# An eighth of a softmax's tokens moved onto the partitions in a four-layer fused network

## The chip, the cores and the metric

One NeuronCore of a Trainium2 chip runs the whole network in one program. The metric is device time in microseconds; three runs of the kernel before took 5653.28, 5671.16 and 5692.56 us, a median of 5671.16. The engines are called PE (TensorE; PEld is its weight load), DVE (VectorE), ACT (ScalarE), POOL (GpSimd) and SP (SyncE, which here only issues DMAs).

## The reference

Sixteen images of 64x64 tokens (4096) with 256 channels pass through four layers. Each layer first normalises its input over 32 groups of channels and adds its result to it. Layer 0 replaces each token by the nearest of 1024 codes, layer 1 is a row-wise attention with a sigmoid, layer 3 a linear attention of four heads with a layer norm. The change concerns layer 2:

```python
    def _L2_conv_ref(x, w1, b1, w2, b2, w3, b3):
        ...
        n = h * w
        xf = x.reshape(b, n, c)
        x0 = jnp.einsum('bnc,c->bn', xf, w1) + b1[0]
        x1 = jnp.einsum('bnc,c->bn', xf, w2) + b2[0]
        x2 = jnp.einsum('bnc,c->bn', xf, w3) + b3[0]
        sim = x0[:, :, None] * x1[:, None, :]
        sm = jax.nn.softmax(sim, axis=1)
        feats = jnp.einsum('bn,bnm->bm', x2, sm)
        gate = jax.nn.sigmoid(feats).reshape(b, h, w, 1)
        return gate * x
```

For each token m, a softmax over all 4096 tokens n of the product x0[n] * x1[m] weighs x2[n]. So an image needs 4096 x 4096 exponentials, their sum over n (the denominator) and their sum weighted with x2 (the numerator).

## The kernel before

The kernel is written with Tile: the code allocates tiles from pools and issues instructions, and a scheduler puts in the waits and fixes the order on each engine. Each layer of each image is a Python generator (stats0 L313, stage1 L329 for layer 0, layer1 L441, rows2 L567, stage2 L620 and gate2 L681 for layer 2, stage3 L717). A generator yields a number after each step, and the main loop at the end interleaves all generators by these numbers: each task has a start and a length in units of one image, so that in the middle of the run layer 0 of one image, layer 1 of the one before, layer 2 of an earlier one and layer 3 of a still earlier one run side by side. Blocks marked as urgent (statistics, small weights) are moved ahead. The engines themselves take their instructions in the resulting order.

PSUM is split into two pools: ps_m with four single banks (`bank`, L70) for most products, and ps_w with two pairs of banks (`wide`, L73). The pairs are used by the search of layer 0 (pd, L403, 32 per image, read by DVE in L409), by layer 1's h (ph, L493, eight per image, read by ACT in L502) and by its output (po, L533, eight per image, read by DVE in L538).

Layer 2 in detail. rows2 computes the three rows x0, x1, x2 for all tokens (L593; four column groups of PE, 32 columns each), writes them to DRAM (L599) and transposes them so that x0 and x1 also stand with the token on the partition, as x01 with 32 tiles of 128 tokens (L602, L603). spread_rows (L610) loads half of the x0 row and half of the x2 row, 2048 tokens each, onto all 128 partitions (L615). stage2 first finds the largest and the smallest x0 (L626, L627, L629), and from them nmax, minus the largest exponent of each token m (L631, L632). Then, for each half of the tokens n and each of the 32 tiles T of tokens m, with m on the partitions and n along the free dimension:

```python
                    nc.scalar.activation(
                        ex, x0b, AF.Exp, bias=nmax[:, T : T + 1], scale=x01[:, T, 1:2], accum_out=den[:, h, T : T + 1]
                    )
                    nc.vector.tensor_tensor_reduce(
                        out=ex, in0=ex, in1=x2b, scale=1.0, scalar=0.0, op0=ALU.mult, op1=ALU.add,
                        accum_out=num[:, h, T : T + 1],
                    )
                    yield 2.4
```

So ACT forms the exponentials and the denominator (L645), DVE multiplies by x2 and forms the numerator (L648), 64 pairs of 2048 columns per image. The sums of both halves give the gate (L656 to L663), which is transposed and stored (L666 to L669). For the last image stage2 runs in eight parts of four tiles T, so that its gate2 can start early.

Other lines that the prediction's steps name: the Identity of layer 0's search (L398), the index search (L414), the gather of codes (L415, an indirect DMA on POOL's queue), layer 1's narrow products (L482) and the bf16 product that adds a bias row (L498), layer 3's key maximum, exponential and context (L754, L774, L803, L809, L813), its transposes (L902) and its output copy (L913).

## Time and profile before

The profiled execution took 5674.06 us, of which the span from the first to the last instruction is 5672.1 us.

| what | value |
|---|---|
| three runs, median | 5671.16 us (5653.28 to 5692.56) |
| profiled execution, span | 5674.06 us, 5672.1 us |
| instructions | 76096 |
| mean granted PE clock | 0.962 of full speed |
| DMA | 1059.26 MB, mean 187 GB/s |
| DVE, layer 2's numerator (L648) | 2360.4 us, 1024 instructions |
| ACT, layer 2's exponentials (L645) | 2138.6 us, 1024 instructions |
| ACT, reading their sums (L645) | 194.4 us, 1024 instructions |
| PE, the search's products (L403) | 1971.1 us, 4096 records |
| DVE, the search (L409 and L414) | 619.9 and 622.9 us, 512 instructions each |
| ACT, the search (L398) | 582.5 us, 512 instructions |

How to read it: the profile gives for each engine the time in which it was busy, and for each group of instructions (line, engine, operation) the busy time, the mean duration of one and the idle time of the engine ahead of them. Matmuls are pipelined, so the records of PE overlap and a busy PE isn't PE at its peak. A product of f32 operands on PE appears as two records. The time of an image in the middle of the run is read from the instruction that occurs once per image, POOL's reduction over partitions (L629): it starts at 1624.26, 1947.51, 2279.78, 2612.22, 2947.67, 3283.12, 3623.10, 3957.20, 4288.91, 4622.80 and 4948.66 us, and for the last image at 5220.89 us.

### The profile page before, as it was taken

What the parts mean: (1) busy time and instruction counts of PE and PEld (TensorE: products, weight loads), DVE (VectorE), ACT (ScalarE), POOL (GpSimd) and SP (SyncE); (2) the same over time, 40 slices, a digit from 0 to 9 for tenths busy, and PEclk for the clock granted to TensorE, in tenths of its full rate; (3) what the DMA queues carried; (4) which work ended last, traced back from release to release, by engine and by line L of the source; (5) the groups of instructions that cost most, each with busy time, mean ns of one, the idle gap of its engine ahead of it and who ended that gap; (6) DMA issues with size and microseconds to landing.
All of it is one profiled execution on the core that took longest, in us unless ns stands there. A gap on an engine that the chain in (4) does not pass through costs nothing.

```text
span 5672.1 us, 76096 instructions
## 1 busy us (share of the span) xinstructions
PE 5162.0 (91%) x26927; PEld 3189.6 (56%) x26927; DVE 5049.3 (89%) x7186; ACT 4571.1 (81%) x6642; POOL 1801.5 (32%) x1076
## 2 busy tenths in 40 slices
PE   7977889989999999999999999999999999987788
PEld 3534446545656566565655656565565656564556
DVE  7589799899999999999999999999999999988882
ACT  4468589888989898888978888898888879887873
POOL 2223234323333333334333333333333333321221
PEclk9988999999999999999999999999999999998889
DMA  8553744655665757566575656657575675745543
GB/s 254 174 178 84 232 115 144 214 163 185 196 198 175 224 159 236 171 211 198 185 234 155 216 185 200 210 173 236 160 224 183 201 219 156 222 149 176 200 157 119
DMA packets 521365, 1059.26 MB, mean 187 GB/s; under 512 B 52504, under 2 KB 266392, under 8 KB 512792
## 3 DMA queue, kind: packets, MB, share of 16 engines
q1 hardware_dynamic: 406288, 885.11, 46.5%
q0 software_dynamic: 73728, 67.14, 8.3%
q10 hardware_dynamic: 40968, 102.13, 4.6%
q8 instruction: 214, 3.51, 0.3%
q14 instruction: 167, 1.37, 0.1%
HBM read 751.18 MB, written 303.04 MB: 186 GB/s over the span
## 4 chain that ended last, share of the span: by engine, by line
PE 46%; DVE 17%; ACT 16%; issue 6%; DMA 5%; POOL 4%; SPq 0%; ACTq 0%; DVEq 0%; POOLq 0%
PE pd_s L403 14%; ACT ex_s L645 7%; DVE ex_s L648 7%; PE ph_l L493 4%; PE pxo_s L908 3%; PE pqv_s L782 3%; PE po_l L533 2%; PE pk_s L765 2%; ACT nn_s L398 2%; POOL qv_s L802 2%; PE pz_s L857 2%; DVE i_s L414 2%; DVE nn_s L409 2%; PE pxo_s L902 2%; PE pvr_s L865 2%
## 5 line engine op out<-in xcount | busy, mean ns | idle before, releaser
L648 DVE CUSTOM_DVE_ANT_0 ex_s<-ex_s,x2b 128x2048 f32<-128x2048 f32 x1024 | 2360.4, 2312 | 77.6 <-ACT ex_s L645 74.6
L645 ACT ACTIVATE ex_s<-x0b,nmax_s,x_r 128x2048 f32<-128x2048 f32 x1024 | 2138.6, 2089 | 40.7 <-DVE num_s L648 30.5
L403 PE MATMUL pd_s<-e,xn_s 128*128 128x512 f32 x4096 | 1971.1, 614 | 43.9 <-DVE m L409 27.9
L415 POOL DMA_INDIRECT xc_s<-in_emb_rows,i_s x512 | 1113.7, 2175 | 1852.7 <-DVE i_s L414 1337.5
L403 PEld LDWEIGHTS pd_s<-e,xn_s 128*128 128x128 f32 x4096 | 745.8, 195 | 778.8 <-issue 669.1
L409 DVE CUSTOM_DVE_ANT_0 nn_s<-pd_s,nn_s 128x1024 f32<-128x1024 f32 x512 | 619.9, 1212 | 113.5 <-PE pd_s L403 63.0
L414 DVE FIND_INDEX8 i_s<-m,nn_s 128x8 uint32<-128x1024 f32 x512 | 622.9, 1217 | 0.0
L398 ACT ACTIVATE nn_s<-ne,nx_s 128x1024 f32<-128x1024 f32 x512 | 582.5, 1143 | 33.1 <-DVE nx_s L369 18.7
L493 PE MATMUL ph_l<-wh_l,xt_l 128*128 128x256 f32 x2048 | 519.6, 390 | 28.7 <-DVE m L409 16.9
L782 PE MATMUL pqv_s<-wqv_s,xk_s 128*128 128x256 f32 x2048 | 489.3, 381 | 0.0
L493 PEld LDWEIGHTS ph_l<-wh_l,xt_l 128*128 128x128 f32 x2048 | 379.7, 192 | 138.9 <-issue 69.0
L782 PEld LDWEIGHTS pqv_s<-wqv_s,xk_s 128*128 128x128 f32 x2048 | 389.1, 191 | 120.6 <-issue 59.7
L802 POOL TENSOR_TENSOR qv_s<-qv_s,qm_s 128x512 f32<-128x512 f32 x128 | 221.6, 1731 | 662.6 <-DVE qm_s L801 363.2
L868 POOL TENSOR_TENSOR lrs_s<-lrs_s,mhalf 128x4 f32<-128x4 f32 x128 | 178.0, 1391 | 677.2 <-ACT lrs_s L867 663.3
L756 POOL TENSOR_TENSOR qv_s<-qv_s,qd_s 128x512 f32<-128x512 f32 x128 | 214.4, 1675 | 249.0 <-DVE qd_s L755 132.0
L533 PE MATMUL po_l<-blk,h_l 128*128 128x128 f32 x2048 | 282.1, 288 | 3.0 <-DVE m L409 1.5
L533 PEld LDWEIGHTS po_l<-blk,h_l 128*128 128x128 f32 x2048 | 260.6, 200 | 41.1 <-issue 24.5
L908 PE MATMUL pxo_s<-wctx_s,qo_s 128*128 128x256 f32 x1024 | 269.2, 386 | 2.2 <-DVE qo_s L876 2.2
L765 PE MATMUL pk_s<-xk_s,wk_s 128*128 128x512 f32 x512 | 256.0, 620 | 1.0 <-DMA xk_s<-x_g 0.9
L913 ACT COPY y_s<-pxo_s 128x512 f32<-128x512 f32 x256 | 147.5, 580 | 132.4 <-PE pxo_s L912 116.0
L378 PE MATMUL pt_s<-ident,xc_s 128*128 128x128 f32 x1024 | 156.7, 282 | 105.2 <-DMA xc_s<-in_emb_rows,i_s 79.0
L351 ACT ACTIVATE sq_s<-xt_s,first 128x512 f32<-128x512 f32 x256 | 200.2, 806 | 37.2 <-DMA x0b<-rows_r 21.0
(206 smaller groups left out, 7322.0 us busy)
## 6 DMA issues: line engine op xcount, KB each, us to landing
xs_s<-in_xT SPq DMA_DIRECT2D x128, 512.0 KB
xt_s<-in_xT SPq DMA_DIRECT2D x128, 512.0 KB
xc_s<-in_x SPq DMA_DIRECT2D x128, 512.0 KB
x_s<-xt_s ACTq DMA_DIRECT2D x128, 512.0 KB
xt_l<-x_s SPq DMA_DIRECT2D x128, 512.0 KB
x_l<-xt_l SPq DMA_DIRECT2D x128, 512.0 KB
xr_r<-x_l SPq DMA_DIRECT2D x128, 512.0 KB
xg_g<-x_l SPq DMA_DIRECT2D x128, 512.0 KB
```

Source lines behind the costliest of these rows:

```text
L398: nc.scalar.activation(nn, ne2, AF.Identity, bias=nx2[ch][:, t : t + 1])
L403: nc.tensor.matmul(pd[:, cols], lhsT=xn[ch][:, k, t * P : (t + 1) * P], rhs=e2[:, k, cols], start=(k == 0), stop=(k == NK - 1),)
L409: nc.vector.tensor_tensor_reduce(out=nn, in0=pd, in1=nn, scale=1.0, scalar=-3.0e38, op0=ALU.add, op1=ALU.max, accum_out=m8[:, 0:1],)
L414: nc.vector.max_index(i8, m8, nn)
L415: nc.gpsimd.indirect_dma_start(out=xc[ch][:, t, :], out_offset=None, in_=emb_rows, in_offset=bass.IndirectOffsetOnAxis(ap=i8[:, 0:1], axis=0),
L493: nc.tensor.matmul(ph[:, t, :], lhsT=X[:, k, t * P : (t + 1) * P], rhs=wh_n[:, k, :], start=(t % 2 == 0 and k == 0), stop=False, skip_grou ...
L533: nc.tensor.matmul(po[:, m : m + P], lhsT=h[:, t, k * P : (k + 1) * P], rhs=at[:, t, :, :].rearrange("p r i -> p (r i)"), start=True, stop ...
L645: nc.scalar.activation(ex, x0b, AF.Exp, bias=nmax[:, T : T + 1], scale=x01[:, T, 1:2], accum_out=den[:, h, T : T + 1])
L648: nc.vector.tensor_tensor_reduce(out=ex, in0=ex, in1=x2b, scale=1.0, scalar=0.0, op0=ALU.mult, op1=ALU.add, accum_out=num[:, h, T : T + 1],)
L765: nc.tensor.matmul(pk, lhsT=wk_n[:, k, :], rhs=xt[:, k, :], start=(k == 0), stop=(k == NK - 1))
L782: nc.tensor.matmul(pqv[:, j, :], lhsT=xt[:, k, t * P : (t + 1) * P], rhs=wqv_n[:, k, :], start=(j == 0 and k == 0), stop=False, skip_group ...
L908: nc.tensor.matmul(px[:, j, :], lhsT=qT[:, t * P : (t + 1) * P], rhs=wctx[:, 1, :], start=False, stop=False, skip_group_check=True,)
```

## The change

Of the 32 tiles of 128 tokens n, the last four (SHARE = 4, an eighth) leave the loop over n along the free dimension. For them n lies on the partitions and m along the free dimension:

- rows2 now also keeps x2 in x01. stage2 gathers x1, nmax and the four tiles of x0 in one tile, transposes it (one PE product), and splits the 68 resulting rows into three bf16 parts each (five DVE instructions on PSUM). They go to DRAM in seven DMAs and come back as the two operands of a product with 12 rows: three rows for nmax against ones, nine for the products of the parts of x0 and x1. All these DMAs are issued on SP's queue.
- Per chunk of 512 tokens m (eight per image), `begin` loads the moving operand (four DMAs on SP, one per row group of PE). `outer`, twice, forms the exponents of two tiles of n in a pair of banks (two bf16 products in two row groups), and `powers` takes the Exp of the pair in one ACT instruction of 1024 columns. `contract` forms both sums over n by four f32 products onto 32 columns each, with x2 and ones as the weights, and copies the bank with ACT; `collect` transposes the result (four PE products) and adds the four groups (one DVE reduction).
- The exponentials and numerators of the second half become 1536 columns wide instead of 2048, and so do the loads of x0 and x2 for it.
- The pairs of banks come from ps_w, the others from ps_m. The two final sums of the gate become reductions over three terms.

The calls hang in the loop of stage2: of each eight steps, outer follows the exponential in steps 0 and 1, powers in steps 1 and 2, contract and the next begin stand in step 5, collect in step 7.

```diff
@@ -37,6 +37,9 @@
 LAG4 = 0.04
 LEN3 = {0: 0.4, 1: 0.33, 2: 0.37}
 FILL = ((0.05, 0.95, 2), (1.0, 1.27, 3), (1.4, 1.58, 2))
+SHARE = 4
+SHARES = {}
+PROD = 12
 EARLY = sum(n for _, _, n in FILL)
 
 
@@ -136,6 +139,14 @@
                 t[:, :512], lhsT=ones3, rhs=ones3.unsqueeze(1).to_broadcast([P, 4, P]), start=True, stop=True,
                 skip_group_check=True,
             )
+
+    spread = const.tile([P, 2, P], BF16, name="spread")
+    nc.gpsimd.memset(spread, 0.0)
+    for g in range(4):
+        nc.gpsimd.memset(spread[32 * g : 32 * g + PARTS], 1.0)
+    pair = const.tile([P, 8, 32], F32, name="pair")
+    nc.gpsimd.memset(pair, 0.0)
+    nc.gpsimd.memset(pair[:, :, 1], 1.0)
 
     h_row, qv_row, x_row = row_tile("h_row"), row_tile("qv_row"), row_tile("x_row")
 
@@ -581,7 +592,7 @@
                 )
             brow_n = small.tile([P, 1], F32, tag="brow_n", name=f"brow_{tag}")
             nc.scalar.activation(brow_n, pb[:, 0:1], AF.Identity, bias=brow)
-        x01 = small.tile([P, NT, 2], F32, tag="x01", name=f"x01_{tag}", bufs=2)
+        x01 = small.tile([P, NT, 3], F32, tag="x01", name=f"x01_{tag}", bufs=2)
         rd = dram.tile([3, 2, 4, CW], F32, tag="rows", name=f"rows_{tag}", bufs=3)
         for h in range(2):
             pr = bank(f"pr_{tag}_{h}")
@@ -602,20 +613,22 @@
                 nc.tensor.transpose(pt[:, t * P : (t + 1) * P], rows[:, t * P : (t + 1) * P], ident)
             nc.vector.tensor_copy(
                 x01[:, 16 * h : 16 * h + 16, :].rearrange("p (j t) n -> p j t n", t=CH),
-                pt.rearrange("p (t j n) -> p j t n", j=4, n=32)[:, :, :, 0:2],
+                pt.rearrange("p (t j n) -> p j t n", j=4, n=32)[:, :, :, 0:3],
             )
             yield 4
         rows_d[b] = x01, rd, [spread_rows(rd, b, 0)]
 
     def spread_rows(rd, b, h):
 
-        x0b = s2p.tile([P, TOK // 2], F32, tag="x0b", name=f"x0b_{b}_{h}", bufs=2)
-        x2b = s2p.tile([P, TOK // 2], F32, tag="x2b", name=f"x2b_{b}_{h}", bufs=2)
-        for dst, n in ((x0b, 0), (x2b, 2)):
+        width = TOK // 2 - (P * SHARES.get(b, SHARE) if h == 1 else 0)
+        both = []
+        for tag, n in (("x0b", 0), ("x2b", 2)):
+            dst = s2p.tile([P, TOK // 2], F32, tag=tag, name=f"{tag}_{b}_{h}", bufs=2)[:, :width]
             nc.sync.dma_start(
-                out=dst, in_=rd[n : n + 1, h, :, :].rearrange("o j n -> o (j n)").to_broadcast([P, TOK // 2])
+                out=dst, in_=rd[n : n + 1, h, :, :].rearrange("o j n -> o (j n)")[:, :width].to_broadcast([P, width])
             )
-        return x0b, x2b
+            both.append(dst)
+        return both
 
     def stage2(b, parts=1):
 
@@ -627,36 +640,136 @@
         nc.vector.tensor_reduce(ext[:, 1:2], x01[:, :, 0], AX.X, ALU.min, negate=True)
         ab = small.tile([P, 2], F32, tag="ab", name=f"ab_{tag}", bufs=1)
         nc.gpsimd.partition_all_reduce(ab, ext, P, bass_isa.ReduceOp.max)
-        nmax = small.tile([P, NT], F32, tag="nmax", name=f"nmax_{tag}", bufs=1)
+        K = SHARES.get(b, SHARE)
+        cat = small.tile([P, 2 * NT + 8], F32, tag="cat", name=f"cat_{tag}", bufs=1)
+        nmax = cat[:, NT : 2 * NT]
         nc.vector.tensor_scalar(nmax, x01[:, :, 1], ab[:, 0:1], -1.0, ALU.mult, ALU.mult)
         nc.vector.scalar_tensor_tensor(nmax, x01[:, :, 1], ab[:, 1:2], nmax, op0=ALU.mult, op1=ALU.min)
-        den = small.tile([P, 2, NT], F32, tag="den", name=f"den_{tag}", bufs=1)
-        num = small.tile([P, 2, NT], F32, tag="num", name=f"num_{tag}", bufs=1)
+        sums = small.tile([P, 2, 3, NT], F32, tag="sums", name=f"sums_{tag}", bufs=1)
         halves.append(spread_rows(rd, b, 1))
+
+        others, banks = {}, {}
+
+        def parts_of_rows():
+            nc.vector.tensor_copy(cat[:, 0:NT], x01[:, :, 1])
+            nc.vector.tensor_copy(cat[:, 2 * NT : 2 * NT + K], x01[:, NT - K :, 0])
+            nc.vector.tensor_copy(pair[:, 0:K, 0], x01[:, NT - K :, 2])
+            n = 2 * NT + K
+            pp = bank(f"pcat_{tag}")
+            nc.tensor.transpose(pp[:n, :P], cat[:, :n], ident)
+            bits = small.tile([2 * NT + 8, PARTS, P], BF16, tag="bits", name=f"bits_{tag}", bufs=1)
+            for m in range(PARTS):
+                nc.vector.tensor_copy(bits[:n, m, :], pp[:n, :P])
+                if m + 1 < PARTS:
+                    nc.vector.tensor_tensor(pp[:n, :P], pp[:n, :P], bits[:n, m, :], ALU.subtract)
+            ud = dram.tile([1 + PARTS, PARTS, NT, P], BF16, tag="ud", name=f"ud_{tag}")
+            nc.sync.dma_start(out=ud[0].rearrange("m t p -> t m p"), in_=bits[NT : 2 * NT])
+            for m in range(PARTS):
+                nc.sync.dma_start(out=ud[1 + m].rearrange("m t p -> t m p"), in_=bits[0:NT])
+            vd = dram.tile([PARTS, PARTS, 8, P], BF16, tag="vd", name=f"vd_{tag}")
+            for m in range(PARTS):
+                nc.sync.dma_start(out=vd[:, m, 0:K].rearrange("m t p -> t m p"), in_=bits[2 * NT : n])
+            for g in range(4):
+                nc.sync.dma_start(
+                    out=spread[32 * g + PARTS : 32 * g + PROD, 0 : K // 4, :],
+                    in_=vd.rearrange("i m (e g) p -> (i m) g e p", g=4)[:, g, 0 : K // 4, :],
+                )
+            return ud
+
+        def begin(c):
+            u = s2p.tile([P, CW], BF16, tag="uu", name=f"uu_{tag}_{c}", bufs=2)
+            src = ud.rearrange("i m t p -> (i m) (t p)")[:, c * CW : (c + 1) * CW]
+            for g in range(4):
+                nc.sync.dma_start(out=u[32 * g : 32 * g + PROD, :], in_=src)
+            others[c] = u
+
+        def outer(c, n):
+            e, q = divmod(n, 2)
+            if n == 0:
+                others[c] = [others.pop(c)]
+            u = others[c][0]
+            pw = wide(f"pet_{tag}_{c}_{n}")
+            for r in range(2):
+                g = 2 * q + r
+                rows = slice(32 * g, 32 * g + PROD)
+                nc.tensor.matmul(
+                    pw[:, r * CW : (r + 1) * CW], lhsT=spread[rows, e, :], rhs=u[rows, :], start=True, stop=True
+                )
+            banks[c, n] = pw
+
+        def powers(c, n):
+            e, q = divmod(n, 2)
+            if q == 0:
+                others[c].append(s2p.tile([P, TOK // 2], F32, tag="ex", name=f"et_{tag}_{c}_{e}", bufs=3))
+            nc.scalar.activation(others[c][-1][:, 2 * q * CW : 2 * (q + 1) * CW], banks.pop((c, n)), AF.Exp)
+
+        def contract(c):
+            pn = bank(f"pn_{tag}_{c}")
+            for e in range(K // 4):
+                for g in range(4):
+                    nc.tensor.matmul(
+                        pn[32 * g : 32 * g + 32, :], lhsT=pair[:, 4 * e + g, :],
+                        rhs=others[c][1 + e][:, g * CW : (g + 1) * CW], start=(e == 0), stop=(e == K // 4 - 1),
+                    )
+            nc.scalar.copy(others[c][-1][:, 0:CW], pn)
+
+        def collect(c):
+            row = others.pop(c)[-1]
+            pt = bank(f"pnt_{tag}_{c}")
+            for t in range(CH):
+                nc.tensor.transpose(pt[:, t * P : (t + 1) * P], row[:, t * P : (t + 1) * P], ident)
+            nc.vector.tensor_reduce(
+                sums[:, :, 2, c * CH : (c + 1) * CH].rearrange("p r t -> p t r"),
+                pt.rearrange("p (t j n) -> p t n j", j=4, n=32)[:, :, 0:2, :], AX.X, ALU.add,
+            )
+
+        if K:
+            ud = parts_of_rows()
+            begin(0)
         gd = dram.tile([NT, P], F32, tag="gate", name=f"gd_{tag}")
         gates_d[b] = gd
         yield 2
         rest = gate2(b) if parts > 1 else None
         for part in range(parts):
             those = range(part * NT // parts, (part + 1) * NT // parts)
+            step = 0
             for h, (x0b, x2b) in enumerate(halves):
                 for T in those:
-                    ex = s2p.tile([P, TOK // 2], F32, tag="ex", name=f"ex_{tag}_{h}_{T}", bufs=3)
+                    width = x0b.shape[-1]
+                    ex = s2p.tile([P, TOK // 2], F32, tag="ex", name=f"ex_{tag}_{h}_{T}", bufs=3)[:, :width]
                     nc.scalar.activation(
-                        ex, x0b, AF.Exp, bias=nmax[:, T : T + 1], scale=x01[:, T, 1:2], accum_out=den[:, h, T : T + 1]
+                        ex, x0b, AF.Exp, bias=nmax[:, T : T + 1], scale=x01[:, T, 1:2],
+                        accum_out=sums[:, 1, h, T : T + 1],
                     )
                     nc.vector.tensor_tensor_reduce(
                         out=ex, in0=ex, in1=x2b, scale=1.0, scalar=0.0, op0=ALU.mult, op1=ALU.add,
-                        accum_out=num[:, h, T : T + 1],
+                        accum_out=sums[:, 0, h, T : T + 1],
                     )
-                    yield 2.4
+                    yield 2.4 * width / (TOK // 2)
+                    c = part + step // 8
+                    n = step % 8
+                    if K == 0:
+                        pass
+                    elif n <= K // 2:
+                        if n > 0:
+                            powers(c, n - 1)
+                            yield 1.2
+                        if n < K // 2:
+                            outer(c, n)
+                    elif n == 5:
+                        contract(c)
+                        if c + 1 < NCHUNK:
+                            begin(c + 1)
+                    elif n == 7:
+                        collect(c)
+                    step += 1
             n = len(those)
             cols = slice(those[0], those[0] + n)
             gate = small.tile([P, NT], F32, tag="gate", name=f"gate_{tag}_{part}", bufs=1)[:, 0:n]
-            nc.vector.tensor_tensor(gate, den[:, 0, cols], den[:, 1, cols], ALU.add)
+            nc.vector.tensor_reduce(gate, sums[:, 1, 0 : 2 + (K > 0), cols].rearrange("p h t -> p t h"), AX.X, ALU.add)
             nc.vector.reciprocal(gate, gate)
             nsum = small.tile([P, NT], F32, tag="nsum", name=f"nsum_{tag}_{part}", bufs=1)[:, 0:n]
-            nc.vector.tensor_tensor(nsum, num[:, 0, cols], num[:, 1, cols], ALU.add)
+            nc.vector.tensor_reduce(nsum, sums[:, 0, 0 : 2 + (K > 0), cols].rearrange("p h t -> p t h"), AX.X, ALU.add)
             nc.vector.tensor_tensor(gate, gate, nsum, ALU.mult)
             nc.scalar.activation(gate, gate, AF.Exp, scale=-1.0)
             nc.vector.tensor_scalar(gate, gate, 1.0, None, ALU.add)
```

## The prediction

> **What bounds the kernel now.** I read the totals first, then the chain of waits, the busy times by stage, the costliest groups and the order of time on TensorE.
>
> ```profile
> PE 5162.0 (91%) x26927; PEld 3189.6 (56%) x26927; DVE 5049.3 (89%) x7186; ACT 4571.1 (81%) x6642; POOL 1801.5 (32%) x1076
> PE 46%; DVE 17%; ACT 16%; issue 6%; DMA 5%; POOL 4%; SPq 0%; ACTq 0%; DVEq 0%; POOLq 0%
> ```
>
> The first line is the busy time of each engine, the second the chain that ended last. No engine stands alone: TensorE and VectorE are both nearly full, ScalarE follows, and the chain runs through TensorE most. The stages, cut where an image's partition_all_reduce (L629, once per image) ran, show where that holds. Columns: window, length, then busy time and records of PE, PEld, DVE, ACT, POOL; the last row is one of the 200 us windows.
>
> ```profile
> 316.69:704.28 387.59, 301.95 (x1320) 154.41 (x1318) 335.16 (x466) 277.17 (x357) 108.68 (x59) 0.90 0.53 161
> 704.28:1624.26 919.98, 857.40 (x4492) 513.97 (x4492) 859.32 (x1179) 807.10 (x1132) 306.68 (x169) 0.97 0.57 175
> 1624.26:4948.66 3324.40, 3143.36 (x16787) 1959.55 (x16786) 3114.89 (x4410) 2840.94 (x4131) 1144.56 (x656) 0.99 0.63 196
> 5220.89:5672.10 451.21, 360.43 (x1728) 259.99 (x1726) 295.19 (x459) 283.37 (x468) 103.47 (x76) 0.88 0.46 155
> ...
> 1800.00:2000.00 200.00, 193.93 (x1031) 120.28 (x1030) 188.41 (x267) 168.57 (x245) 69.75 (x43) 0.98 0.69 217
> ```
>
> The stretch from 1624 to 4949 us is ten images of 332.4 us. Of each, PE is busy 314.3 us (94.6%), DVE 311.5 (93.7%), ACT 284.1 (85.5%). The 200 us window is the fullest that PE gets after the start: 97%.
>
> **What the change removes.** Layer 2's exponents of the second half of the tokens become 1536 wide instead of 2048, 32 pairs per image.
>
> ```profile
> L648 DVE CUSTOM_DVE_ANT_0 ex_s<-ex_s,x2b 128x2048 f32<-128x2048 f32 x1024 | 2360.4, 2312 | 77.6 <-ACT ex_s L645 74.6
> L645 ACT ACTIVATE ex_s<-x0b,nmax_s,x_r 128x2048 f32<-128x2048 f32 x1024 | 2138.6, 2089 | 40.7 <-DVE num_s L648 30.5
> L409 DVE CUSTOM_DVE_ANT_0 nn_s<-pd_s,nn_s 128x1024 f32<-128x1024 f32 x512 | 619.9, 1212 | 113.5 <-PE pd_s L403 63.0
> ```
>
> VectorE: the same operation takes 2.312 us at 2048 and 1.212 at 1024, 1.07 ns a column; 512 columns are 0.55 us, 17.6 us per image. ScalarE: exponentials take 2.089 us at 2048 and 0.628 at 512 (L803), 0.95 ns a column; 0.487 us each, 15.6 us per image.
>
> **What it adds on VectorE.** Eight reductions of 32 values per partition: between the copy of that size (L603, 0.174 us) and the reduction of 512 (L754, 0.678); nearer the copy, 0.2, so 1.6. Once per image the splitting of 68 rows into three bf16 parts: three copies (nearest L813, 0.292) and two subtractions (nearest L809, 0.340), with three small copies 2.1; the final sums, now reductions, 0.2. Together 3.9 (3.5 to 8), net -13.7 us per image.
>
> **On ScalarE.** Sixteen exponentials of 1024 columns from a pair of banks: the copy of that shape takes 1.013 (L502), the Exp of 512 from a bank 0.670 (L774), plus 0.487 is 1.16; I take 1.1, so 17.6. Eight copies of a bank at 0.58 (L913), 4.6. Net +6.6 (+5 to +8). At 85.5% ScalarE has room for it.
>
> **On TensorE.** Per image: sixteen bursts of two bf16 products with 12 rows and 512 columns (outer), eight bursts of four f32 products onto 32 columns each (contract), 32 transposes, one more for the parts. The rows are the order of time on PE (start, length, engine, line, operation, xcount; an f32 product is two records):
>
> ```profile
> 3705.43 1.07 PE L482 MATMUL pfg_l<-xt_l,wfg_l 128*32 128x256 f32 x16
> 3706.43 1.13 PE L493 MATMUL ph_l<-wh_l,xt_l 128*128 128x256 f32 x4
> 3707.40 0.38 PE L498 MATMUL ph_l<-h_row,ones 128*128 128x512 bf16 x1
> 3707.62 1.89 PE L493 MATMUL ph_l<-wh_l,xt_l 128*128 128x256 f32 x8
> ...
> 2593.82 1.94 PE L593 MATMUL pr_r<-xr_r,wrow_n 128*32 128x512 f32 x16
> 2595.69 2.84 PE L403 MATMUL pd_s<-e,xn_s 128*128 128x512 f32 x6
> ```
>
> A bf16 product of 512 columns holds PE 0.22 us (3707.40 to 3707.62; the rest of its 0.38 overlaps). The 16 narrow records of L482 hold it 1.00 where four at a time would stream 0.86, and the four full ones behind take 1.13 instead of 1.03 elsewhere: about 0.24 for going into the narrow form and out of it. Outer: 0.22 if the two row groups stream together, 0.43 if in turn, and 0.24 for the switch; I take 0.56, the middle of 0.46 and 0.67, 9.0 us per image. Contract: L593's 16 records hold PE 1.87, so eight 0.94 and the way out, 1.0; one after the other eight records of 0.43 are 3.4. L593 is the same shape in the same four column groups, so 1.0: 8 us per image. The transposes cost 0.44 per four (L902), with the one for the parts 3.8. Together 21 us per image. The lower bound, no switch and everything side by side, is 14; the upper, contract in turn and outer 0.67, is 42.
>
> [...]
>
> **Waits.** Each outer takes one of two bank pairs, so far used 48 times per image (32 by L403, 8 each by ph and po), now 64. The pair is held until ScalarE's exponential, which the code puts behind the next 2 us Exp, about one of the 64 steps of 332 us: 5 us. What queues behind a PE waiting for a pair is every stage's products. Today that wait is small (waits view: engine, line, releaser, total, times, longest):
>
> ```profile
> PE ph_l L493 <- DVE m L409: 13.7, 7, 2.0
> ...
> PE pd_s L403 <- DVE m L409: 1.4, 2, 1.1
> ```
>
> The two come to 1.5 us per image in the stretch; I put a growth of 2 us inside the margin below. SP gets 43 more issues per image, at about 0.37 us each (the nearest rows) 16 us, and two store-then-load waits, where today such a wait (x0b on its rows) totals 43.1 us in 24 times, 1.8 each. Behind them stand the loads of the search, layer 1 and layer 3. These load about two chunks ahead, a chunk being 332/8 = 41 us, so I cost it at nothing; with the cover gone, 10 us per image, 160 in all. GpSimd gets only memsets at the start, 1 us.
>
> **The sum.** The profiled execution took 5674.1 us with a span of 5672.1, 3 us above the median of the three runs. In the stretch PE goes to 314.3 + 21 = 335.3 us, more than the whole period of 332.4. At the 97% of its fullest window that is 345.7, +13.3 over ten images: +133. From 704 to 1624 (three of 306.7, PE 285.8): 306.8/0.97 = 316.3, +9.6 three times: +29. From 317 to 704 and after 5221 PE is at 78 and 80% and the saved 13.7 us count; about half of it each, as VectorE is not alone there: -12. With the start +1: 5674 + 151 = **5825 us**. By its own bounds: 14 us instead of 21 gives 328.3/0.97 = 338.5, +61 and +7, less 12, 5730; PE no fuller than today's 94.6% gives 354.4, +220, and in the earlier stretch at 93.2% 329, +67, 5960; 42 us on PE at 97% gives 367 and 338, +350 and +94, about 6110.
>
> **Rivals.** *VectorE was the bound, and PE's busy time is slack (faster).* Records overlap: counting 0.43 us per 512 columns of an f32 record, 0.215 per 256 and so on, the products of one image need only about 297 us of PE, 89% of the period, and the rest is tails at waits. VectorE at 311.5 - 13.7 = 297.8 and today's 93.7% would allow 317.8. PE needs 297 + 14 = 311 at the least, which at 97% is 320.6: -12 for each of ten images, -11 for each of three, -30 at the ends: 5490. With 21 us it is 318/0.97 = 328, some -85 in all, 5590. Nearer the second I put it at **5580**. It decides if outer and contract cost PE less than about 17 us. Against it: the chain is 46% PE and 17% DVE, and PE in order of time runs for tens of us with no gap.
>
> [...]
>
> *It evens out.* 13.7 off VectorE, 21 onto an engine with 35 us of tails and idle per image: about **5670**.
>
> *Bank pairs.* Each second outer makes a product wait as long as the mean of the row above, 1.96 us: 16 us per image, +200 over thirteen, **6020**. It decides if pairs are held well over 5 us, because ScalarE gets behind.
>
> **How the numbers follow.** About 1% is what a measurement of this kernel can tell from no change: 5614 to 5728. Forecast (PE the bound) 0.56, of which 0.03 within 1%; VectorE the bound 0.22; even 0.12; bank pairs 0.10. So faster 0.22, same 0.15, slower 0.63. The range, 5570 to 6010, leaves out the lower half of the second case and what lies above PE no fuller than now: most of the bank pairs and contract in turn. The forecast's own range is 5730 to 5960.
>
> **What would show it.** Right: in the middle PE busy near 97%, DVE under 90%, a period near 346 us, contract about 1 us, DVE waiting for PE more than now. Wrong: a period under 330 with PE's records the same, or outer's two products starting together and nothing lost around them (faster); or a large wait of the search's products for the new exponential, or loads arriving late (slower still).

## The result and the profile after

Four runs of the changed kernel took 5979.96 to 5991.99 us, median 5990.2; four of the kernel before 5653.28 to 5692.56, median 5673.14. The ratio is 1.0552 [1.0521, 1.0583]: 5.5% slower, 317 us. The span of the profiled execution grew from 5672.1 to 5986.8 us.

Totals, chain and stages of the kernel after, with the same columns as before (stages: window, length, busy time and records of PE, PEld, DVE, ACT, POOL, then PE clock, DMA share, GB/s):

```profile
PE 5480.0 (92%) x28991; PEld 3291.3 (55%) x28991; DVE 4850.2 (81%) x7442; ACT 4673.2 (78%) x7026; POOL 1729.2 (29%) x1083
PE 52%; DVE 11%; ACT 8%; issue 4%; DMA 3%; POOL 1%; POOLq 0%; ACTq 0%; DVEq 0%; SPq 0%
```

```profile
319.10:712.36 393.26, 322.04 (x1457) 160.68 (x1457) 321.35 (x482) 286.15 (x384) 106.93 (x59) 0.90 0.53 159
712.36:1705.98 993.62, 917.05 (x4834) 533.73 (x4833) 818.41 (x1215) 817.42 (x1192) 286.11 (x168) 0.96 0.52 162
1705.98:4886.74 3180.76, 3006.83 (x16294) 1819.25 (x16292) 2704.62 (x4134) 2617.32 (x3940) 1010.36 (x592) 0.98 0.59 186
5456.08:5986.80 530.72, 436.60 (x2168) 304.18 (x2166) 332.35 (x545) 351.08 (x589) 96.13 (x85) 0.88 0.46 151
```

The third row of stages is nine images between the same reductions over partitions. The same nine images of the kernel before, for comparison, since the prediction's row held ten:

```profile
1624.26:4622.80 2998.54, 2834.70 (x15123) 1767.15 (x15122) 2812.95 (x3987) 2558.89 (x3723) 1029.64 (x592) 0.98 0.63 197
```

An image takes 353.4 us instead of 333.2, +20.2. Of the busy times of an image, PE grew by 19.1 us (315.0 to 334.1), DVE fell by 12.0 (312.6 to 300.5), ACT grew by 6.5 (284.3 to 290.8). PE's busy share is 94.5% in both. At first sight the time follows PE's work to the microsecond; the experiments show that this is a coincidence.

The 314.7 us of span by stage: up to the first image's reduction +2.4, the next stage +5.7, the three images +73.6 (24.5 each), the nine +182.2, the tenth +20.9 (325.9 to 346.8), and the two last together +29.8 (272.2 to 222.6 and 451.2 to 530.7).

The groups that answer to those of before, and the Exp of the pair of banks (busy time, mean ns, idle time ahead of it and its main releaser):

```profile
L744 DVE CUSTOM_DVE_ANT_0 ex_s<-ex_s,x2b 128x2048 f32<-128x2048 f32 (+1 forms) x1024 | 2073.2, 2034 | 157.8 <-ACT ex_s L740 156.7
L740 ACT ACTIVATE ex_s<-x0b,cat_s,x_r 128x2048 f32<-128x2048 f32 (+1 forms) x1024 | 1920.1, 1876 | 66.8 <-DVE sums_s L744 60.5
L420 DVE CUSTOM_DVE_ANT_0 nn_s<-pd_s,nn_s 128x1024 f32<-128x1024 f32 x512 | 621.8, 1215 | 300.4 <-PE pd_s L414 217.8
...
L704 ACT ACTIVATE et_s<-pet_s 128x1024 f32<-128x1024 f32 x256 | 260.6, 1019 | 81.7 <-PE pet_s L695 80.4
```

The removed work is gone as computed. VectorE waits more: its idle time ahead of the search went from 113.5 us (63.0 of it for PE's products) to 300.4 (217.8), and ahead of the numerators, nearly all for ACT's Exp, from 77.6 to 157.8. PE's waits in the nine images after:

```profile
PE pgt_s L779 <- DVE gate_s L776: 45.1, 9, 9.6
PE pt_s L389 <- DMA xc_s<-in_emb_rows,i_s: 28.1, 9, 3.6
...
PE pd_s L414 <- DVE m L420: 19.4, 17, 1.4
...
PE pet_s L695 <- DMA spread<-vd_s: 10.9, 9, 2.1
```

The first is new in this stretch: once per image, 5.0 us, PE stands at the transposition of the gate. The last is the new load of the weights of outer. Of the two bank-pair waits of the prediction's rows, pd for m has grown from 1.1 us in nine images to 19.4, and ph for m, 11.8 before, is gone.

The two new shapes in PE's order of time (start, length, engine, line, operation, records):

```profile
3303.68 0.39 PE L695 MATMUL pet_s<-uu_s,spread 12*128 12x512 bf16 x2
3304.05 3.70 PE L414 MATMUL pd_s<-e,xn_s 128*128 128x512 f32 x8
...
3328.24 1.06 PE L710 MATMUL pn_s<-et_s,pair 128*32 128x512 f32 x8
3329.24 0.65 PE L988 MATMUL pdv_s<-ident,lrs_s 128*128 128x128 f32 x4
```

From start to next start outer holds PE 0.37 us here and contract 1.00.

### The profile page after: what moved, and what is told of

The parts are those of the page before. It is cut to its first block, busy times and chain, and to the rows that moved or that the text cites. A ratio compares the mean times of both kernels' runs of the same rounds, so it can differ in the third digit from the quotient of the medians.

```text
span 5986.8 us, 81555 instructions
## 1 busy us (share of the span) xinstructions
PE 5480.0 (92%) x28991; PEld 3291.3 (55%) x28991; DVE 4850.2 (81%) x7442; ACT 4673.2 (78%) x7026; POOL 1729.2 (29%) x1083
## 4 chain that ended last, share of the span: by engine, by line
PE 52%; DVE 11%; ACT 8%; issue 4%; DMA 3%; POOL 1%; POOLq 0%; ACTq 0%; DVEq 0%; SPq 0%
PE pd_s L414 15%; DVE ex_s L744 5%; PE ph_l L504 4%; PE pqv_s L895 4%; PE pxo_s L1021 3%; ACT ex_s L740 3%; PE pk_s L878 3%; PE po_l L544 2%; PE pn_s L710 2%; PE pxo_s L1015 2%; PE pz_s L970 2%; PE pvr_s L978 2%; PE pc_s L920 2%; PE pfg_l L493 1%; DMA xc_s<-in_emb_rows,i_s 1%
## 5 line engine op out<-in xcount | busy, mean ns | idle before, releaser
L744 DVE CUSTOM_DVE_ANT_0 ex_s<-ex_s,x2b 128x2048 f32<-128x2048 f32 (+1 forms) x1024 | 2073.2, 2034 | 157.8 <-ACT ex_s L740 156.7
L740 ACT ACTIVATE ex_s<-x0b,cat_s,x_r 128x2048 f32<-128x2048 f32 (+1 forms) x1024 | 1920.1, 1876 | 66.8 <-DVE sums_s L744 60.5
L420 DVE CUSTOM_DVE_ANT_0 nn_s<-pd_s,nn_s 128x1024 f32<-128x1024 f32 x512 | 621.8, 1215 | 300.4 <-PE pd_s L414 217.8
L409 ACT ACTIVATE nn_s<-ne,nx_s 128x1024 f32<-128x1024 f32 x512 | 579.1, 1143 | 61.0 <-DVE nx_s L380 40.4
L981 POOL TENSOR_TENSOR lrs_s<-lrs_s,mhalf 128x4 f32<-128x4 f32 x128 | 201.6, 1575 | 666.5 <-ACT lrs_s L980 649.0
L915 POOL TENSOR_TENSOR qv_s<-qv_s,qm_s 128x512 f32<-128x512 f32 x128 | 169.8, 1326 | 746.4 <-DVE qm_s L914 527.2
L704 ACT ACTIVATE et_s<-pet_s 128x1024 f32<-128x1024 f32 x256 | 260.6, 1019 | 81.7 <-PE pet_s L695 80.4
L878 PE MATMUL pk_s<-xk_s,wk_s 128*128 128x512 f32 x512 | 274.2, 662 | 0.7 <-DMA xk_s<-x_g 0.7
L869 POOL TENSOR_TENSOR qv_s<-qv_s,qd_s 128x512 f32<-128x512 f32 x128 | 152.8, 1194 | 415.3 <-DVE qd_s L868 290.9
L544 PE MATMUL po_l<-blk,h_l 128*128 128x128 f32 x2048 | 265.5, 280 | 5.9 <-DVE m L420 3.2
L544 PEld LDWEIGHTS po_l<-blk,h_l 128*128 128x128 f32 x2048 | 247.0, 193 | 32.6 <-issue 17.2
```

Source lines behind the costliest of these rows:

```text
L409: nc.scalar.activation(nn, ne2, AF.Identity, bias=nx2[ch][:, t : t + 1])
L420: nc.vector.tensor_tensor_reduce(out=nn, in0=pd, in1=nn, scale=1.0, scalar=-3.0e38, op0=ALU.add, op1=ALU.max, accum_out=m8[:, 0:1],)
L544: nc.tensor.matmul(po[:, m : m + P], lhsT=h[:, t, k * P : (k + 1) * P], rhs=at[:, t, :, :].rearrange("p r i -> p (r i)"), start=True, stop ...
L740: nc.scalar.activation(ex, x0b, AF.Exp, bias=nmax[:, T : T + 1], scale=x01[:, T, 1:2], accum_out=sums[:, 1, h, T : T + 1],)
L744: nc.vector.tensor_tensor_reduce(out=ex, in0=ex, in1=x2b, scale=1.0, scalar=0.0, op0=ALU.mult, op1=ALU.add, accum_out=sums[:, 0, h, T : T ...
L878: nc.tensor.matmul(pk, lhsT=wk_n[:, k, :], rhs=xt[:, k, :], start=(k == 0), stop=(k == NK - 1))
```

## The experiments

Two theories at the start. *PE's work*: the time follows the 19 us of products that an image gets, and PE can't be filled further. *Waits*: the products could be borne, but what hangs on them (readers on ScalarE and VectorE, the gate, the loads) makes engines stand. Percentages of PE are its busy share in the nine images between the same reductions; "above" is the median above that of the kernel before measured with it.

**The relief alone.** The share is left out, and with it an eighth of the tokens of each sum.

```diff
-SHARE = 4
+SHARE = 0
-        width = TOK // 2 - (P * SHARES.get(b, SHARE) if h == 1 else 0)
+        width = TOK // 2 - (P * 4 if h == 1 else 0)
```

> The last four tiles of n are left out altogether: no share on TensorE, and the second half stays 1536 wide, so VectorE loses 17.6 us and ScalarE 15.6 us per image against the kernel before, TensorE nothing (the gate then lacks an eighth of its sums). If TensorE's own work sets the period (314.97 us busy of 333.2), little is to be had: 5560 to 5640 us. If VectorE set it (312.6 busy), the period follows its 17.6 us: 5430 to 5480 us.

5543.27 us, 0.9773 [0.9756, 0.9789]: 130 below, between the two expectations. PE's products are the same and PE goes from 94.5 to 96.4%. So PE alone did not set the time before. The edit takes 14.1 us an image off ScalarE and 14.7 off VectorE together, so it doesn't say which of the two counted.

**The share without the relief.** All second halves stay 2048 wide, the third sum is formed and not added to the gate's two; the weights of the steps stay those of the change.

```diff
-        width = TOK // 2 - (P * SHARES.get(b, SHARE) if h == 1 else 0)
+        width = TOK // 2
```

> The share is computed in full but not used, and the second half stays 2048 wide: TensorE's added work without VectorE's and ScalarE's relief. If TensorE sets the period after the change, the relief was worth nothing there: 5980 to 6070 us. If the relief was needed to pay part of the share, about 17 us per image more: 6170 us and above.

6071.84 us, 1.0696 [1.0676, 1.0715]: 399 above, just over the upper end of the first expectation. With the share in place the relief gives back only 82 us, and the share itself costs 399. That is what has to be taken apart.

**PE's work alone.** The kernel before, with the first product of the search done twice in 22 of 32 tiles, once into a bank that is begun anew behind it.

```diff
+                    if hf == 0 and T % 3 != 2:
+                        nc.tensor.matmul(
+                            pd[:, cols], lhsT=xn[ch][:, 0, t * P : (t + 1) * P], rhs=e2[:, 0, cols], start=True, stop=True
+                        )
```

> The kernel before with one of the search's products issued twice in 22 of 32 tiles: 22 x 0.86 = 18.9 us more of TensorE per image, as much as the share's measured 19.1, with no new buffer, no new hand-over between engines and no DMA. If products alone make the loss, most of it appears: 5930 to 5980 us. If the loss is the new waits (bank pairs, spread, gate, gather), the products alone cost less than half: below 5800 us.

5791.49 us, 1.0218 [1.0194, 1.0241]: 118 above. The nine images:

```profile
1667.80:4733.26 3065.46, 2987.82 (x15543) 1832.67 (x15542) 2837.90 (x3985) 2563.94 (x3726) 1002.41 (x593) 0.99 0.61 193
```

PE got 17.0 us more per image (2987.82 against 2834.70, over nine), and the image grew by 7.4: PE fills to 97.5%. The products alone don't explain 317 us, and less than half of an added product's time shows.

**The gate's transposition later.** The changed kernel, with the step between the gate's reciprocal and its transposition on PE longer.

```diff
-            yield 1
+            yield 5 if parts == 1 else 1
```

> The changed kernel with the transpose of the gate four units (about 8 us of the plan) later. TensorE's wait for the gate (45.1 us in nine images) should go. If the wait costs what it shows plus the slow products behind it (672 against 597 ns for the key products), 7 to 8 us per image: 5860 to 5900 us. If TensorE's idle time only moves to another wait, 5960 us or more.

5920.72 us, 1.0431 [1.0407, 1.0456]: 70 below the changed kernel, between the two expectations. Some 66 of it lie in the nine images, which take 346.1 us each instead of 353.4. PE's waits for the gate in the whole run, first of this kernel and then of the changed one:

```profile
PE pgt_s L779 <- ACT kx_s L887: 18.6, 11, 5.8
PE pgt_s L779 <- DVE gate_s L776: 17.4, 7, 5.9
```

```profile
PE pgt_s L779 <- DVE gate_s L776: 73.2, 21, 9.6
```

These fell by 37 us, the time by more. In the last of the 64 steps the last collect and its reduction now stand ahead of the gate's sums; the transposition came too early for that.

The same edit in the kernel before:

> The kernel before with the gate's transpose four units later. Its wait there is small (11.2 us in all), so 5660 to 5690 us if the wait is what e4 took away; below 5640 us if the later place is better by itself.

5698.54 us (ten runs), 1.003 [1.0015, 1.0045], somewhat more than expected: there the wait does not exist in the middle, and moving the step costs 17 us. The wait is the change's own.

**One exponential buffer less.** et comes from the three buffers "ex" of the exponentials and keeps one from step 1 to step 7 of every eight. In the kernel before:

```diff
-                    ex = s2p.tile([P, TOK // 2], F32, tag="ex", name=f"ex_{tag}_{h}_{T}", bufs=3)
+                    ex = s2p.tile([P, TOK // 2], F32, tag="ex", name=f"ex_{tag}_{h}_{T}", bufs=2)
```

> The kernel before with two buffers for layer 2's exponentials instead of three. In the changed kernel the share's exponentials take one of those three for six of eight steps. If that lost buffer is a large part of the loss, 5760 to 5850 us here; if VectorE and ScalarE run apart well enough with two, within 15 us of the kernel before.

5723.14 us, 1.0072 [1.0048, 1.0096]: 46 above, between the two expectations. Only some 10 of it lie in the nine images (334.3 us each instead of 333.2); most is lost in the four images before them (1345.5 us against 1307.6). VectorE's wait for exponentials in the whole run has doubled; first here, then in the kernel before (total, times, longest):

```profile
DVE ex_s L648 <- ACT ex_s L645: 148.3, 132, 4.0
```

```profile
DVE ex_s L648 <- ACT ex_s L645: 74.6, 66, 2.8
```

In the changed kernel the same wait stands at 156.7. ScalarE's own wait for a numerator that still holds a buffer went from 30.5 us to 43.0 here, and stands at 60.5 in the changed kernel. That the changed kernel's waits are due to the buffer is likely, not shown.

**Holding things for a shorter time.** Two tries on the kernel with the late gate: contract and collect earlier, which frees the buffer in step 4; and the Exp of the pair straight behind the next exponential.

```diff
-                    elif n == 5:
+                    elif n == 3:
                         contract(c)
...
-                    elif n == 7:
+                    elif n == 4:
                         collect(c)
```

> The kernel with the late gate (5920.7 us), and contract in step 3 instead of 5, collect in step 4 instead of 7: the shared buffer is held from step 1 to 4 instead of 1 to 7. If the lost buffer matters, half of its price comes back: 5840 to 5890 us. If it does not, 5910 to 5940 us.

```diff
+                    if K and 0 < n <= K // 2:
+                        powers(c, n - 1)
+                    yield 2.4 * width / (TOK // 2)
...
-                            powers(c, n - 1)
```

> The kernel with the late gate, and the exponential of a pair put straight behind the next step's Exp, without the plan's 5 us between: the bank pair is held about 5 us less. If held pairs keep the search's products waiting, 5840 to 5890 us; if not, 5900 to 5940 us.

5950.28 us, 1.0477 [1.0458, 1.0496], and 5923.77, 1.044 [1.0422, 1.0458], against 5920.72 without. That is 273 and 247 above, where the late gate was 247. The first is 26 us *slower*, though the buffer is free sooner; the second changes nothing. A shorter hold of a pair or buffer gains nothing here, and a mere change of order is worth 26 us.

**No chain of loads.** The late-gate kernel, but the parts, their stores and all loads of operands only for the first image; every chunk of every image reads those, so all other thirds of the sums are those of other exponents.

```diff
-        if K:
+        if K and b == 0:
             ud = parts_of_rows()
...
         def begin(c):
-            u = s2p.tile([P, CW], BF16, tag="uu", name=f"uu_{tag}_{c}", bufs=2)
...
+            others[c] = kept["u"]
```

> The kernel with the late gate; the splitting into parts, the stores and the loads of spread and the moving operand run for the first image alone and all chunks read that one operand (so the gate's third term is that of other exponents). TensorE's products for exponents and sums all remain. If the chain of DMAs on SP and the waits behind it (spread, the loads of tokens, the gather) are a large part, 5790 to 5860 us; if the loads were hidden, as the prediction put it, 5900 us or more.

5865.88 us, 1.0333 [1.0316, 1.035]: 189 above, 59 less than with the late gate alone and just over the upper end of the first expectation.

**Down to the products, and up again.** The share without relief and with the late gate, reduced to its products: constant operands, no reader of any result, no parts, no DMAs (the third sums are left out). Then readers are added.

```diff
         def begin(c):
...
+            others[c] = moving
...
-            nc.scalar.activation(others[c][-1][:, 2 * q * CW : 2 * (q + 1) * CW], banks.pop((c, n)), AF.Exp)
+            banks.pop((c, n))
...
-            nc.scalar.copy(others[c][-1][:, 0:CW], pn)
```

> The share without relief (second half 2048 wide), its products only: outer, contract and collect run at their places in the same forms and banks, on constant operands, and nothing reads what they write (no exponential of the pairs, no copy, no reduction, no parts, no DMAs; the gate as before, four units later). If TensorE's time alone is what these products cost, as for the doubled search products, 5770 to 5820 us. If short bursts in other forms cost more than their time, 5860 us or more.

5760.68 us, 1.0148 [1.0117, 1.0179]: 79 above, PE at 97.3%.

All readers back, from constant operands, into buffers of their own (the Exp of the pairs, the copy, the transposes of the copy, the reduction):

```diff
+            if q == 0:
+                others[c].append(s2p.tile([P, 2 * CW], BF16, tag="et", name=f"et_{tag}_{c}_{e}", bufs=1))
+            nc.scalar.activation(others[c][-1], banks.pop((c, n)), AF.Exp)
...
+            others[c].append(s2p.tile([P, CW], F32, tag="er", name=f"er_{tag}_{c}", bufs=1))
+            nc.scalar.copy(others[c][-1], pn)
```

> The same with the readers back: ScalarE's exponentials of the pairs and copies of the sums (22 us per image), VectorE's reductions, in buffers of their own, so that the main exponentials keep all three. Against e9 this prices ScalarE's added work and the hand-overs between engines. If ScalarE has room for them, as the prediction put it, within 25 us of e9; if they are what is still missing from the loss, 90 us or more above it.

5917.92 us, 1.0422 [1.039, 1.0453]: 237 above. The nine images of the two, products alone first:

```profile
1649.27:4706.76 3057.49, 2974.64 (x16310) 1810.29 (x16309) 2837.65 (x3990) 2561.46 (x3730) 1005.11 (x592) 0.99 0.62 194
```

```profile
1681.07:4814.75 3133.68, 3005.11 (x16289) 1815.97 (x16288) 2852.26 (x4063) 2716.72 (x3942) 1062.11 (x592) 0.99 0.60 189
```

With the same products PE falls from 97.3 to 95.9% and the image grows by 8.5 us, which is 76 us in the nine images. In the whole run 157 us come from reading alone. Is it ScalarE's time, or the hand-over from one engine to the other? First, ScalarE reads only 32 columns of each pair and of the sums (the transposes take a constant, and a small one more takes the copy):

```diff
-            nc.scalar.activation(others[c][-1], banks.pop((c, n)), AF.Exp)
+            nc.scalar.activation(others[c][-1][:, 0:32], banks.pop((c, n))[:, 0:32], AF.Exp)
```

> e10 with all hand-overs kept, but ScalarE reads 32 columns of each pair and of each bank of sums instead of 1024 and 512 (one more small transpose waits for that copy): about 17 us per image less of ScalarE. If ScalarE's added time is what its readers cost, near the products alone: 5770 to 5810 us. If it is the hand-overs, near e10: 5890 us or more.

5956.83 us, 1.0476 [1.0454, 1.0499]: 278 above, no better with three quarters of the readers' time on ScalarE taken away, even 42 us worse. The nine images:

```profile
1686.45:4871.27 3184.82, 3019.04 (x16353) 1834.45 (x16352) 2844.81 (x4056) 2585.65 (x3935) 1084.13 (x593) 0.98 0.60 186
```

ScalarE is busy 2.7 us more per image than with the products alone, and an image takes 14.2 more. The converse is products without readers, and ScalarE's full time on a constant:

```diff
+            nc.scalar.activation(others[c][-1], ne2, AF.Exp)
             banks.pop((c, n))
...
+            nc.scalar.copy(others[c][-1], ne2[:, 0:CW])
```

> e9 with ScalarE's added time back but reading a constant in SBUF: no hand-over between TensorE and ScalarE or VectorE, nobody reads what the products write. If ScalarE's added time is the cost, near e10: 5880 to 5930 us. If it is the hand-overs, near e9: 5760 to 5800 us.

5770.45 us, 1.0148 [1.0125, 1.0172]: 92 above, the same ratio as the products alone. By these two the hand-over would be the price. Then one hand-over at a time on top, of the pair, and of the sums with the reduction behind the transposes:

```diff
-            nc.scalar.activation(others[c][-1], ne2, AF.Exp)
-            banks.pop((c, n))
+            nc.scalar.activation(others[c][-1], banks.pop((c, n)), AF.Exp)
```

> e13 with one hand-over back: ScalarE's exponential reads the pair that outer wrote. The sums of contract are still read by nobody. If the pair's hand-over carries the loss, 5880 to 5930 us; if that of the sums does, 5770 to 5800 us.

```diff
-            nc.scalar.copy(others[c][-1], ne2[:, 0:CW])
+            nc.scalar.copy(others[c][-1], pn)
...
-            row = e2[:, 0, :]
+            row = others.pop(c)[-1]
```

> e13 with the other hand-over back: ScalarE copies the sums of contract, TensorE transposes that copy, VectorE reduces it; the exponentials read a constant. If the sums carry the loss, 5880 to 5930 us; if the pair does, 5770 to 5810 us.

5853.2 us, 1.0307 [1.0271, 1.0343], and 5819.15, 1.0245 [1.021, 1.028]: 82 and 48 us more than the stream alone, which seemed to confirm it. But nothing held the constant stream in its place: it was loose, free for the scheduler to move. The windows of its Exps alone (window, length, busy time and records, then clock, DMA share, GB/s):

```profile
0.00:320.00 320.00, 98.99 (x94) 0.96 0.71 213
...
4712.00:5200.00 488.00, 0.00 (x0) 0.97 0.56 172
```

94 of 256 had moved into the first 320 us, where ScalarE is busy 139 us in the run of the products alone, and none was left for the end. But what stood in the middle tells more than that. The nine images:

```profile
1647.94:4712.36 3064.42, 2973.21 (x16296) 1808.85 (x16295) 2842.60 (x3987) 2657.13 (x3855) 997.18 (x593) 0.99 0.63 193
```

ScalarE works 10.6 us more per image than with the products alone, and the image takes 0.8 more. In five images in a row (1992.00 to 3686.89 us) 73 of their 80 Exps stand: ScalarE works 300.4 us per image, against 284.4 in the same five with the products alone (1987.43 to 3685.22), and the image takes 339.0 us against 339.6. Loose, 16.0 us of ScalarE's time cost nothing there. So the stream was given its place: each Exp and copy takes its scale from the sum that ScalarE itself has formed one instruction earlier.

```diff
-            nc.scalar.activation(others[c][-1], ne2, AF.Exp)
+            nc.scalar.activation(others[c][-1], ne2, AF.Exp, scale=sums[:, 1, h, T : T + 1])
...
-            nc.scalar.copy(others[c][-1], ne2[:, 0:CW])
+            nc.scalar.activation(others[c][-1], ne2[:, 0:CW], AF.Identity, scale=sums[:, 1, h, T : T + 1])
```

> Leaves out the third sums, as the run with the stream alone. There, 94 of the 256 Exps and 46 of the 128 copies on the constant ran in the first 320 us, since nothing held them back. Here each takes its scale from the sum that ScalarE has just formed in the step before, so the stream stands in its place. Theory that ScalarE's time is free: 5755 to 5785 us, as with the stream moved forward (1.0148). Theory that ScalarE's time is the price: 5850 us or more, most of the way to the 1.0422 of all readers, and then the hand-overs cost little.

5923.85 us, 1.0429 [1.0411, 1.0447]: 248 above, 169 more than the products alone, with no hand-over at all. Of the two groups, the Exps and the copies, the idle time ahead is 0.3 us in the whole run each:

```profile
L676 ACT ACTIVATE et_s<-ne,sums_s 128x1024 bf16<-128x1024 f32 x256 | 292.7, 1143 | 0.3
L688 ACT ACTIVATE er_s<-ne,sums_s 128x512 f32<-128x512 f32 x128 | 91.6, 716 | 0.3
```

The nine images:

```profile
1700.66:4824.24 3123.58, 2991.05 (x16271) 1819.38 (x16270) 2834.34 (x3985) 2741.28 (x3938) 1028.48 (x594) 0.98 0.60 189
```

ScalarE has 20.0 us more per image than with the products alone (2741.28 against 2561.46, over nine), the image takes 7.3 us more, and PE is at 95.8%: a loss like that of all the readers, from ScalarE's stream alone once it is tied to its place. Now the same two edits as above, one each, on top of this (the other part of the stream stays in its place on the constant):

> Leaves out the third sums. As the stream in its place, but the Exp reads the pair of banks; the copy stays on the constant. Theory that the hand-over costs: 50 to 90 us above the stream in its place. Theory that ScalarE's time is the price: within 25 us of the stream in its place.

> Leaves out the third sums. As the stream in its place, but the copy reads the sums, the transposes read the copy and the reduction reads the transposes; the Exps stay on the constant. Theory that the hand-over costs: 35 to 70 us above the stream in its place. Theory that ScalarE's time is the price: within 25 us of it.

5892.3 us, 1.0376 [1.0358, 1.0393], and 5879.83, 1.0363 [1.0345, 1.038]: 32 and 44 us *less* than the stream in its place. That is outside the ranges of both theories. The instructions that read banks are shorter, by 33 and 17 us over the run (1016 ns for 1143, 582 for 716). Nor do the hand-overs add up: both together, the run with all readers, stand at 237 above, 20 and 32 more than either alone (217 and 204).

So neither theory of the readers holds by itself. The hand-over isn't needed for the loss (the stream in its place), and ScalarE's time is neither enough (the loose stream, 16.0 us an image for nothing) nor, as far as one run tells, needed (the narrow readers, 2.7 us for 14.2). What the runs that lose have in common is 24 more instructions per image that stand at fixed places in ScalarE's order, tied there by what they read. The loss also grows with their number: 92 above with none tied, 139 with the 8 copies, 173 with the 16 Exps, 204 to 278 with all 24.

## Why the prediction was wrong

The changes of time, in us over the run, by the prediction and by the runs:

| term | prediction | runs | from |
|---|---|---|---|
| products on PE | +162 (133 + 29) | +79 | products alone |
| readers (Exp of the pairs, copy, reduction) | 0 ("has room") | +157 | all readers; +169 for the stream in its place, without hand-over |
| gate's transposition ahead of its data | not in it | +70 | late gate |
| parts, stores and loads | +1 (start) | +59 | no chain |
| a buffer of the exponentials | not in it | +46 | two buffers, kernel before |
| relief | -12 | -82 | share without relief |
| all | +151 | +317 | |

The rows of the runs come from different surroundings, and each edit also changes the order on the engines; they sum to 329. Single terms under some 40 us are not safe: the earlier contract (+26) and the gate's step in the kernel before (+17) show what a mere change of order does. By stages, the ten images were given +133 and took +203, the three before them +29 and +74, and the rest -11 and +38.

*What held.* VectorE -13.7 us an image (measured -12.0), ScalarE +6.6 (+6.5), PE +21 (+19.1); contract "1.0" (1.00); VectorE under 90% (85.0) and waiting for PE more than now; the sign, and a time inside the range. The signs of PE near 97% and a period near 346 us did not come: 94.5% and 353.4. Outer was taken as 0.56 us and holds PE 0.37. The 97% was a fair number for PE's work alone: 97.3 and 97.5% with bare and with doubled products. The bound of 5960 leaves out the 12 us that the other bounds take off.

*The step that failed* is the one on ScalarE: "At 85.5% ScalarE has room for it", and with it the sum, which lets PE alone set the period and puts what ScalarE must read at nothing. The readers cost 157 us. The sentence counted time, and as to time it was right where that was tried: beside the products alone, 16.0 us an image of loose work cost nothing. It didn't ask where the new instructions stand. Tied to their places, 20.0 us an image cost 7.3, and 2.7 us an image cost 14.2. Which wait carries the price stays open: PE's waits in the nine images add up to 78 us with the products alone and to 125, 164 and 127 with all readers, the narrow ones and the stream in its place, spread over several places that differ from run to run. A sign of it stood in the profile of the kernel before: of the 162 us that PE waited in the same nine images, 113 ended with ScalarE.

The second is *Waits*, which went through bank pairs and loads and not through the gate: 70 us. In the middle this is most of what the forecast lacks. An image takes 20.2 us more, 13.3 were forecast, and the late gate takes 7.4 back. That it then takes 346.1, next to the forecast's 345.7, is luck: bare products, the forecast's only cost there, give 339.7.

Two more terms were mis-sized, both so that the forecast came out too long. The products were charged in full (162, where 79 were measured): doubled ones cost 7.4 us an image for 17.0 of PE, bare ones 6.5 for 15.5 (2974.64 against 2834.70, over nine), some 0.4 us for each. And the relief was worth 82 us and not 12. Some 150 us too much for these two stand against some 330 left out. The forecast was 166 us short, and the time came inside the range because these errors partly cancel.

*VectorE was the bound* is true so far as PE was not the only bound: 130 us of relief with PE's work unchanged, 6.9 us an image (333.2 to 326.3). Whether VectorE's 14.7 us or ScalarE's 14.1 earned that was not separated by a run.

*What was not seen* are the other terms, which stand in the code. et has the tag "ex", with three buffers for the exponentials until then. The gate follows the last collect, whose reduction VectorE must do first, while the transposition kept its step on PE. And the loads were looked for at SP's queue ("I cost it at nothing", with 160 us if the cover were gone): with parts and stores, some 59 were due.

*Bank pairs*, at 6020 us the nearest rival in time, is not what happened. Its waits are there (pd for m, 2.2 us an image, where it gave 16), but a shorter hold gains nothing, and reading the pair instead of a constant took 32 us off in one surrounding and added 32 in another (204 to 237 above).

The busy share of PE's weight loads said little of PE's room here: it is 59% in the nine images of before (1767.15/2998.54) and 60% with doubled products (1832.67/3065.46), while PE goes from 94.5 to 97.5%. ScalarE's 85% told its room for loose work rightly (16.0 us an image for nothing), and said nothing of work at fixed places (20.0 us for 7.3).

*Open.* Which wait the tied instructions lengthen is not shown. The narrow readers have only 73 us of ScalarE's time in the run (48.9 and 23.8), and yet were slower than the full ones; the small transposition that waits for the copy, and a wait of the code's transposes for ScalarE of 42.5 us in nine images, are in it, but what it would have cost without them was not tried. No version here beats the kernel before while forming the whole sums: the best of them is the one with the late gate, 4.3% above it.

## What to carry to other kernels

Here three engines at 85 to 95% that hand work to each other had no single bound (130 us went with PE's work unchanged, 118 came with PE's work alone), and the busy share of one didn't price what was added to it: PE's added time showed at some 0.4, and ScalarE's at nothing where it was loose and at 4 to 14 us an image where all of it was tied to its place, and not in step with its length. Ask of each new instruction what it waits for and what stands behind it on its engine. For every tile that a change allocates, ask whose buffers its tag takes, and when a sum gets a later last term, look at the step of whoever waits for it. A stand-in that depends on nothing may be moved by the scheduler to where it is free: look where it ran before reading its time, as the stream alone and the stream in its place differ by some 157 us (92 and 248 above).

## What the runs showed of the hardware

Here a wait of PE cost more than its length. In the changed kernel's order of time, with the idle time and its releaser in brackets:

```profile
2776.64 5.32 PE L414 MATMUL pd_s<-e,xn_s 128*128 128x512 f32 x12
2785.81 0.40 PE L779 MATMUL pgt_s<-ident,gate_s 128*32 128x128 f32 x1 [3.85 <-DVE gate_s L776]
2786.00 3.66 PE L878 MATMUL pk_s<-xk_s,wk_s 128*128 128x512 f32 x4
2789.46 2.79 PE L895 MATMUL pqv_s<-wqv_s,xk_s 128*128 128x256 f32 x8
```

The four products of pk take 3.66 us where the same four take 1.88 at 2443.12 us, at a granted clock of 1.00. The windows around it (the third number from the end is the granted clock):

```profile
2776.00:2782.00 6.00, 5.96 (x20) 2.74 (x18) 5.42 (x16) 4.36 (x5) 3.22 (x3) 1.00 0.32 106
2782.00:2786.00 4.00, 0.19 (x1) 0.19 (x2) 3.51 (x6) 4.00 (x7) 2.25 (x2) 0.81 0.33 47
2786.00:2792.00 6.00, 6.00 (x13) 3.47 (x13) 5.06 (x8) 0.71 (x2) 0.13 (x1) 0.56 0.29 97
2792.00:2800.00 8.00, 7.75 (x45) 5.85 (x43) 4.37 (x11) 6.03 (x12) 2.49 (x2) 1.00 0.63 165
```

After 3.85 us without work the granted clock averages 0.56 over the next six microseconds: the wait cost 3.85 and then another 2.7 (1.8 on pk, 0.9 on pqv, whose eight records take 1.89 at 2444.84 us, at a granted clock of 1.00). Over the run the products of pk keep PE busy for 256.0 us before, 274.2 after, and 253.9 with the late gate, so a wait at one place was paid again by the products behind it. That is some 20 of the 33 us that the late gate gained beyond the waits themselves.
